# Group-norm statistics from transposed blocks, joined by averaging matrices, and the first relative-position products placed between the keys

## The chip, the cores and the metric

The kernel runs on one core of one Trainium2 chip. A core has five engines that run their own instruction streams: TensorE (matrix products, PE in the profile), VectorE (DVE), ScalarE (ACT), GpSimd (POOL) and SyncE (SP), which here issues all the DMA transfers. Working memory (SBUF) has 128 partitions; matrix products land in eight accumulation banks (PSUM). The metric is the device time of one execution in microseconds (us); lower is better. All data are 32-bit floats.

## The reference, cut to what matters

Two images of 48x48 tokens and 768 channels go through an attention layer and then a spectral layer, each behind a group norm of 32 groups of 24 channels:

```python
def _gn(v, G=32, eps=1e-5):
    B_, H_, W_, C_ = v.shape
    g = v.reshape(B_, H_, W_, G, C_ // G)
    m = jnp.mean(g, axis=(1, 2, 4), keepdims=True)
    s = jnp.var(g, axis=(1, 2, 4), keepdims=True)
    return ((g - m) / jnp.sqrt(s + eps)).reshape(v.shape)

# attention, inside
attn = jnp.einsum('bqc,bkc->bqk', q * scale, k)
rel_h = jnp.einsum('bhwc,hkc->bhwk', r_q, Rh)
rel_w = jnp.einsum('bhwc,wkc->bhwk', r_q, Rw)
attn = attn + rel_h[..., None] + rel_w[..., None, :]     # shapes shortened
attn = jax.nn.softmax(attn, axis=-1)
...
x = x + _L0_conv_ref(_gn(x), ...)    # attention
x = x + _L1_conv_ref(_gn(x), ...)    # spectral layer
```

The change concerns the first `_gn`, the one ahead of the attention, and the order of the work that follows it.

## The kernel before, in words

`block_kernel` handles the two images one after the other: `attention`, then `project_out` (which also computes the second group norm's statistics), then `Spectral(...).run`. A tile framework orders the instructions, so the start of image 1's `attention` may interleave with the end of image 0's spectral stage (`ps_u`, `ps_x`, the adds `x<-ps_x` at L968, the stores `out<-x` at L971, the round trip `u_d` and `u` through device memory at L940 and L950). Inside `attention`, from L195 on, the engines are wrapped in `InOrder`: what is issued through `pe`, `dve`, `act` and `sync` keeps its program order, and its line in the profile is L66 (the wrapper's), so these rows are told apart by tile names.

`norm_transpose` (L82 to L135) does the first group norm. Six loads bring `x` as six tiles of 128 partitions x 3 token tiles x 768 channels (`xt`, L103). For each of them and each of six channel blocks (`NCC` = 6) TensorE transposes three 128x128 pieces into one bank `gn_tp` (L109), and ScalarE copies the bank into `xnT` (L113), where channels lie on partitions and the 2304 tokens along the row, in an order by quarters (`stretches`). Some banks take two copies of 192 columns in place of one of 384. Beside this, `tile_stats` (L700) computes, for each of the 18 token tiles, the mean of each group of 24 channels (VectorE, L703 and L704), the centred values (GpSimd, L706), their squares (ScalarE, L709) and the sums of squares (VectorE, L710). `join_stats` (L713) joins tokens and tiles: two products with a matrix of ones (`js_tot`, L720 and L733), some VectorE work on 18x32 columns (`js_off`), square root and reciprocal. `cmask` and `pick` (L119, L123) spread the 32 group values to the 128x6 channel layout, and 18 instructions of 768 columns (L128) normalise `xnT` in place.

After that, `attention` loads the first weights (`load_w`; the third shares its buffer with the second), and computes for head pair 0 the queries of token group 0 (`queries`), six parts of the keys (`keys`), the relative products of group 0 (`relative`: `ps_r`, copied to `rel`), writes them skewed to device memory and reads them back (`write`, `read`: tiles `t` and `rhw`), the queries of group 1, and then the first unit (`new_unit`: GpSimd spreads the two relative terms over the 2304 keys in a tile `s`, one instruction for each of the two heads, L320). The main loop runs over units (head pair, group, third): `scores` (products `ps_s`, added into `s` by VectorE with a running maximum), `numerators` (ScalarE's exponential), transposes and DMA exchanges to `pT`, `weigh` (`ps_o`), with keys and values of the next head pair in between. `evict` writes out what waits on ScalarE.

The few lines that carry the first order of work after the norm:

```python
qT = queries(0, 0)
evict(by_act)
for i in range(6):
    keys(0, i)
    evict(by_act)
rhw, write, read = relative(0, qT)
...
ahead = new_unit(*order[0])
```

A query group needs columns 0 to 1535 of `xnT` for its rows (twelve runs of 32 in the first quarter); a part of the keys needs 384 columns next to each other.

Of the kernel before, what the change touches and what calls it, by code (L numbers as in the profile page):

```python
# [9 lines left out]
F32 = mybir.dt.float32  # L10
AF = mybir.ActivationFunctionType
ALU = mybir.AluOpType
AX = mybir.AxisListType
# [3 lines left out]
P = 128  # L17
HW = 48
S = HW * HW
C = 768  # L20
# [3 lines left out]
NCC = C // P  # L24
NT = S // P
NG = 32
GC = C // NG
# [5 lines left out]
UQ = 384  # L33
# [8 lines left out]
YP = 112  # L42
XP = 4
WP = 5
LAM = 0.01
GN_EPS = 1e-5
LOWEST = -3.0e38
# [21 lines left out]
def stretches(cols, g):  # L69


    by_quarter = cols.rearrange("p (t c j) -> p t c j", c=4, j=32)
    e = 0
    while e < UQ:
        c, t = divmod((g * UQ + e) // 32, NKC)
        n = min(NKC - t, (UQ - e) // 32)
        yield e, e + 32 * n, by_quarter[:, t : t + n, c, :]
        e += 32 * n
# [3 lines left out]
def norm_transpose(nc, k, pools, bank, x_b, xnT):  # L82

    tiles, small, work, a = pools
    k.load(nc, a, small, {"cmask": [P, NCC, NG]})
    local = small.tile([P, NT, NG], F32, tag="local", name="local")  # L90
    dev = small.tile([P, NT, NG], F32, tag="dev", name="dev")
    src = x_b.rearrange("(t p) c -> p t c", p=P)
    loaded = []
    for i in range(NT // 3):
        if i < 2:
            xt = tiles[0].tile([P, S], F32, tag="x", name="xt")
        elif i % 2 == 0:
            both = tiles[1].tile([P, 2, S], F32, tag="s", name="xt")
            xt = both[:, 0, :]
        else:  # L100
            xt = both[:, 1, :]
        xt = xt.rearrange("p (t c) -> p t c", c=C)
        nc.sync.dma_start(out=xt, in_=src[:, 3 * i : 3 * i + 3, :])  # L103
        loaded.append(xt)
    for t0, xt in zip(range(0, NT, 3), loaded):
        for cc in range(NCC):
            tp = bank("gn_tp")
            for i in range(3):
                nc.tensor.transpose(  # L109
                    tp[:, i * P : (i + 1) * P], xt[:, i, cc * P : (cc + 1) * P], k.ident  # L110
                )
            for e0, e1, dst in stretches(xnT[:, cc, :], t0 // 3):
                nc.scalar.copy(dst, tp[:, e0:e1].rearrange("p (t j) -> p t j", j=32))  # L113
        for i in range(3):
            tile_stats(nc, work, xt[:, i, :], local[:, t0 + i, :], dev[:, t0 + i, :])
    cols = []
    for i, stat in enumerate(join_stats(nc, k, small, bank, local, dev)):
        m = small.tile([P, NCC, NG], F32, tag="pick", name="pick")
        nc.vector.tensor_tensor(  # L119
            m, k.cmask, stat[:, None, :].to_broadcast([P, NCC, NG]), ALU.mult  # L120
        )
        c = small.tile([P, NCC], F32, tag=f"gcol{i}", name=f"gcol{i}")
        nc.vector.tensor_reduce(c, m, AX.X, ALU.add)  # L123
        cols.append(c)
    for c0 in range(0, S, 2 * UQ):
        for cc in range(NCC):
            xs = xnT[:, cc, c0 : c0 + 2 * UQ]
            nc.vector.tensor_scalar(  # L128
                xs,
                xs,  # L130
                cols[0][:, cc : cc + 1],
                cols[1][:, cc : cc + 1],
                ALU.subtract,
                ALU.mult,
            )  # L135


# [1 line left out]
def attention(tc, k, x_b, a, oT, inv_d, late, span, ps_b, ps_o):  # L139
# [10 lines left out]
    nc = tc.nc  # L150
    with ExitStack() as ctx:
# [11 lines left out]
        sp = pool("at_s", 3)  # L163
# [19 lines left out]
        rel = relp.tile([P, 2, 3, 2, RW], F32, tag="rel", name="rel")  # L183
        with ExitStack() as ctx2:
            small = ctx2.enter_context(tc.tile_pool(name="gn_s", bufs=1))
            work = lambda name: small.tile([P, C], F32, tag="st", name=name, bufs=2)
            more = ctx2.enter_context(tc.tile_pool(name="gn_x", bufs=2))
            norm_transpose(nc, k, ((more, sp), small, work, a), bank, x_b, xnT)
        ptp = pool("at_pt", 2)
        b_cols = a["qkv_b"].rearrange("(j p) -> p j", p=P)  # L190
        with nc.allow_non_contiguous_dma(reason="biases onto partitions"):
# [21 lines left out]
        by_act, by_dve = [], []  # L213

        def evict(waiting):
            while waiting:
                waiting.pop(0)()
# [234 lines left out]
        groups, weights, kTs, vs = {}, {}, {}, {}  # L452
        for which in (0, 1):
            weights[which] = load_w(which, 0)
        qT = queries(0, 0)
        evict(by_act)
        for i in range(6):
            keys(0, i)
            evict(by_act)
        rhw, write, read = relative(0, qT)  # L460
        evict(by_act)
        write()
        read()
        groups[0, 0] = (qT, rhw)
        weights[2] = load_w(2, 0)
        staged = ((0, 1), queries(0, 1))
        evict(by_act)
        ahead = new_unit(*order[0])
        recent = []
        last = turn = send = None  # L470
        for n in range(len(order) + 3):
# [228 lines left out]
def tile_stats(nc, work, xt, local, dev):  # L700

    x3 = xt.rearrange("p (g d) -> p g d", d=GC)
    nc.vector.tensor_reduce(local, x3, AX.X, ALU.add)  # L703
    nc.vector.tensor_scalar(local, local, 1.0 / GC, None, ALU.mult)  # L704
    xc = work("st_xc").rearrange("p (g d) -> p g d", d=GC)
    nc.gpsimd.tensor_tensor(  # L706
        xc, x3, local[:, :, None].to_broadcast([xt.shape[0], NG, GC]), ALU.subtract
    )
    nc.scalar.activation(xc, xc, AF.Square)  # L709
    nc.vector.tensor_reduce(dev, xc, AX.X, ALU.add)  # L710


def join_stats(nc, k, small, bank, local, dev):  # L713

    ntok = float(S)
    rows, tiles = local.shape[:2]
    part = small.tile([rows, NG], F32, tag="js_part", name="js_part")
    nc.vector.tensor_reduce(part, local.rearrange("p t g -> p g t"), AX.X, ALU.add)
    tot = bank("js_tot")
    nc.tensor.matmul(tot[:, :NG], lhsT=k.ones[:rows, :], rhs=part, start=True, stop=True)  # L720
    mean = small.tile([P, NG], F32, tag="js_mean", name="js_mean")
    nc.vector.tensor_scalar(mean, tot[:, :NG], 1.0 / ntok, None, ALU.mult)
    off = small.tile([rows, tiles, NG], F32, tag="js_off", name="js_off")
    nc.vector.tensor_tensor(
        off, local, mean[:rows, None, :].to_broadcast([rows, tiles, NG]), ALU.subtract
    )
    nc.vector.tensor_tensor(off, off, off, ALU.mult)
    nc.vector.tensor_scalar(off, off, float(GC), None, ALU.mult)
    nc.vector.tensor_tensor(off, off, dev, ALU.add)
    part2 = small.tile([rows, NG], F32, tag="js_part", name="js_part2")  # L730
    nc.vector.tensor_reduce(part2, off.rearrange("p t g -> p g t"), AX.X, ALU.add)
    tot2 = bank("js_tot2")
    nc.tensor.matmul(tot2[:, :NG], lhsT=k.ones[:rows, :], rhs=part2, start=True, stop=True)  # L733
    std = small.tile([P, NG], F32, tag="js_std", name="js_std")
    nc.scalar.activation(std, tot2[:, :NG], AF.Sqrt, bias=k.eps, scale=1.0 / (ntok * GC))
    rstd = small.tile([P, NG], F32, tag="js_rstd", name="js_rstd")
    nc.vector.reciprocal(rstd, std)
    return mean, rstd
# [3 lines left out]
class Spectral:  # L742
# [50 lines left out]
    def bank(self, name):  # L793
        return self.ps_b.tile([P, 512], F32, tag="b", name=name)
# [278 lines left out]
def shape_constants():  # L1073

    h = np.arange(HW)
    full = 2 * np.pi * ((h[:, None] * h[None, :]) % HW) / HW
    half = full[:, :KW]
    s = 1.0 / np.sqrt(HW)

    order = np.concatenate([h[0::2], h[1::2]])  # L1080

    fw = np.zeros((2, HW, KW, 2, 2))
    for i in range(2):
        fw[i, :, :, 0, i], fw[i, :, :, 1, i] = np.cos(half) * s, -np.sin(half) * s
    fw = np.concatenate([fw.reshape(2 * HW, 4 * KW), np.zeros((2 * HW, YP - 4 * KW))], 1)

    co, si = np.cos(full), np.sin(full)
    fh = np.block([[co[order], -si[order]], [si[order], co[order]]]) * s

    ih = np.zeros((2, HW, 2, 2, HW // 2))  # L1090
    for i in range(2):
        c2, s2 = co[:, i::2] * s, si[:, i::2] * s
        ih[0, :, i, 0], ih[1, :, i, 0] = c2, -s2
        ih[0, :, i, 1], ih[1, :, i, 1] = s2, c2
    ih = np.pad(ih.reshape(2, HW, 2 * HW), ((0, 0), (0, 64 - HW), (0, 0))).reshape(P, 2 * HW)

    m = np.full((KW, 1), 2.0)
    m[0] = m[-1] = 1.0
    sin = np.sin(half).T.copy()
    sin[0] = sin[-1] = 0.0  # L1100
    iw = np.zeros((KW, 2, 2, 2, HW))
    for i in range(2):
        iw[:, i, 0, i], iw[:, i, 1, i] = m * np.cos(half).T * s, -m * sin * s
    iw = iw.reshape(4 * KW, 2 * HW)
    gmask = np.arange(BS)[:, None] // GC == np.arange(4)[None, :]
    cmask = (np.arange(C).reshape(NCC, P).T // GC)[:, :, None] == np.arange(NG)
    named = {"cmask": cmask, "fh": fh, "fw": fw, "ih": ih, "iw": iw, "gmask": gmask}
    return {n: np.ascontiguousarray(v, dtype=np.float32) for n, v in named.items()}


# [47 lines left out]
```

## Time and profile before

| what | time in us |
|---|---|
| median of three runs | 3907.91 (3903.24 to 3908.79) |
| profiled execution, its own time | 3910.83 |
| its span in the profile | 3908.9 |
| image 0: first x tile used, last statistics joined, first projection, second score add | 8.0, 54.0, 59.84, 107.23 |
| image 1: first x load issued, first projection, second score add | 1923.25, 2010.48, 2057.03 |
| VectorE busy in 8 to 20 us | 12.00 of 12.00 |
| TensorE busy in 45 to 60 us | 1.38 of 15.00 |

The page of the profile gives the busy time of each engine, the span in 40 slices (a digit is the busy share in tenths), the chain of work that ended last, and the costliest groups of instructions. An "idle before" in a row is what the engine waited for. The chain of waits lists, in order of time, which engine or transfer held up the end at each point. A matrix product of 32-bit floats shows as two records.

### The profile page before, as it was taken

To read this page: it belongs to the slowest core of one execution; us is meant where nothing else is said; L and a number is where in the kernel's file an instruction comes from. 1 tells how busy PE (TensorE), PEld (TensorE's weight loads), DVE (VectorE), ACT (ScalarE), POOL (GpSimd) and SP (SyncE) were. 2 spreads that over 40 slices of the span, in tenths; PEclk is the share of its full clock that TensorE was granted. 3 is DMA by queue.
4 is the path that set the end of the run, shared out by engine and by line. 5 is a ranking of instruction groups with operands and counts; after the bars stand their busy time and mean duration, and the time that the engine had idled before them with its cause. 6 is when DMAs were issued, how large, how long until landed. Compare 5 with 4: busy or idle time off the path is not lost.

```text
span 3908.9 us, 83210 instructions
## 1 busy us (share of the span) xinstructions
PE 3660.4 (94%) x31416; PEld 2591.6 (66%) x31416; DVE 2987.5 (76%) x6642; ACT 2528.1 (65%) x3585; POOL 2117.0 (54%) x682
## 2 busy tenths in 40 slices
PE   6999999999999888989959999999999999779898
PEld 4677776767777655566536777767677776545665
DVE  5688888888889885654546888888888888856544
ACT  3588888888888882222135888888888888722221
POOL 2566666666666666422225666666666666664221
PEclk7999999999999998999989999999999999989999
DMA  2477777777777888534424777777777778884344
GB/s 93 100 169 172 171 175 165 170 172 174 173 167 166 175 197 197 130 84 122 139 85 104 176 171 170 168 174 168 172 172 167 176 164 177 189 197 127 85 121 131
DMA packets 496094, 606.22 MB, mean 155 GB/s; under 512 B 180109, under 2 KB 311053, under 8 KB 495694
## 3 DMA queue, kind: packets, MB, share of 16 engines
q1 hardware_dynamic: 495694, 600.89, 66.1%
q8 instruction: 250, 4.10, 0.5%
q14 instruction: 150, 1.23, 0.1%
HBM read 130.81 MB, written 87.67 MB: 56 GB/s over the span
## 4 chain that ended last, share of the span: by engine, by line
PE 80%; DVE 6%; DMA 6%; POOL 4%; SPq 3%; issue 1%; ACT 1%; POOLq 0%; DVEq 0%; ACTq 0%
PE ps_o L66 20%; PE ps_s L66 19%; PE ps_proj L66 14%; PE ps_v L66 8%; PE acc L670 5%; DVE s L66 4%; PE ps L905 4%; POOL s L320 2%; SPq L66 2%; DMA pT<-s 2%; PE ps_z L853 2%; PE ps L878 2%; PE ps L882 2%; PE ps_u L936 2%; PE ps_r L66 1%
## 5 line engine op out<-in xcount | busy, mean ns | idle before, releaser
L320 POOL TENSOR_TENSOR s<-rhw 128x2304 f32<-128x2304 f32 x432 | 1744.8, 4060 | 1096.4 <-DMA pT<-s 575.9
L66 DVE CUSTOM_DVE_ANT_0 s<-ps_s,s 128x512 f32<-128x512 f32 (+1 forms) x2160 | 1223.3, 633 | 401.0 <-issue 225.6
L66 ACT ACTIVATE s<-s,nm 128x1152 f32<-128x1152 f32 x864 | 1074.7, 1245 | 445.9 <-DVE nm L66 415.1
L66 DVE STREAM_TRANSPOSE s<-s 128x1152 f32<-128x1152 f32 x864 | 1111.8, 1344 | 5.5 <-ACT s L66 5.5
L66 ACT COPY pT<-s 32x1152 f32<-32x1152 f32 x864 | 993.2, 1149 | 28.8 <-PE ps_o L66 13.3
L66 PE MATMUL ps_o<-pT,v 128*64 128x128 f32 x15552 | 924.5, 279 | 77.7 <-DMA pT<-s 41.7
L66 PEld LDWEIGHTS ps_o<-pT,v 128*64 128x64 f32 x15552 | 872.7, 140 | 140.6 <-issue 79.0
L66 PE MATMUL ps_s<-kT,qT 64*128 64x512 f32 (+1 forms) x4320 | 922.4, 559 | 23.2 <-DVE mx L66 19.3
L66 PEld LDWEIGHTS ps_s<-kT,qT 64*128 64x128 f32 x4320 | 432.5, 187 | 462.6 <-issue 335.6
L66 PE MATMUL ps_proj<-xnT,w 128*128 128x384 f32 (+1 forms) x2016 | 597.4, 450 | 11.8 <-issue 11.8
L66 PEld LDWEIGHTS ps_proj<-xnT,w 128*128 128x128 f32 x2016 | 360.5, 191 | 219.2 <-DVE mx L66 41.1
L670 PE MATMUL acc<-proj 128*128 128x384 f32 x864 | 291.6, 497 | 24.5 <-POOL proj L616 12.4
L66 PEld LDWEIGHTS ps_v<-w,xnT 128*128 128x128 f32 x2592 | 297.6, 194 | 21.8 <-DVE mx L66 21.8
L66 PE MATMUL ps_v<-w,xnT 128*128 128x128 f32 x2592 | 309.8, 279 | 0.0
L922 POOL TENSOR_TENSOR spectrum<-spectrum 128x480 f32<-128x480 f32 x80 | 96.2, 1203 | 326.7 <-DVE spectrum L921 323.9
L670 PEld LDWEIGHTS acc<-proj 128*128 128x128 f32 x864 | 168.0, 195 | 144.6 <-issue 21.3
L709 ACT ACTIVATE st_xc<-st_xc 96x768 f32<-96x768 f32 (+1 forms) x84 | 71.1, 847 | 266.7 <-POOL st_xc L706 266.7
L679 DVE TENSOR_TENSOR x<-acc,x 32x384 f32<-32x384 f32 (+2 forms) x216 | 119.5, 553 | 80.2 <-PE acc L670 76.3
L66 DVE DVE_READ_ACCUMULATOR2_ANT mx<- 128x1 f32 x2160 | 180.1, 83 | 0.0
L66 ACT ACTIVATION_READ_ACCUMULATOR s<-s,nm 128x1 f32 x864 | 161.2, 187 | 0.0
L710 DVE TENSOR_REDUCE dev<-st_xc 96x32 f32<-96x768 f32 (+1 forms) x84 | 78.9, 948 | 96.4 <-ACT st_xc L709 96.4
L706 POOL TENSOR_TENSOR st_xc<-x,local 96x768 f32<-96x768 f32 x48 | 70.9, 1481 | 148.2 <-DVE local L704 128.8
(87 smaller groups left out, 2275.1 us busy)
## 6 DMA issues: line engine op xcount, KB each, us to landing
pT<-s SPq DMA_DIRECT2D x2592, 144.0 KB
t<-rel SPq DMA_DIRECT2D x144, 189.0 KB
rhw<-t SPq DMA_DIRECT2D x144, 144.0 KB
y_d<-y SPq DMA_DIRECT2D x24, 672.0 KB
y<-y_d SPq DMA_DIRECT2D x40, 360.0 KB
u_d<-spectrum SPq DMA_DIRECT2D x40, 360.0 KB
u<-u_d SPq DMA_DIRECT2D x48, 300.0 KB
xt<-in_x SPq DMA_DIRECT2D x12, 1152.0 KB
```

The source lines that it names most:

```text
L66: return lambda *args, **kw: self.tc.keep_in_program_order(op(*args, **kw))
L320: nc.gpsimd.tensor_tensor(s[:, h, :].rearrange("p (y x) -> p y x", x=HW), rhw[:, x, h, :HW][:, :, None].to_broadcast([P, HW, HW]), rhw[:, ...
L670: nc.tensor.matmul(acc[:, :UQ], lhsT=o_sb[:, cc, (t % 3) * P : (t % 3 + 1) * P], rhs=pr.w[:, cc, cols], start=(cc == 0), stop=(cc == NCC - 1),
L679: nc.vector.tensor_tensor(dst, acc[p : p + n, :UQ], dst, ALU.add)
L709: nc.scalar.activation(xc, xc, AF.Square)
L710: nc.vector.tensor_reduce(dev, xc, AX.X, ALU.add)
L853: nc.tensor.matmul(ps[:BS, w * 96 : (w + 1) * 96], lhsT=self.y2[s, j][:, w, i * BS : (i + 1) * BS], rhs=k.fh, start=True, stop=True,)
L878: nc.tensor.matmul(ps[:BS, :400], lhsT=w1[:, wa, i, :], rhs=zf[:, 0, fs], start=True, stop=False,)
L882: nc.tensor.matmul(ps[:BS, :400], lhsT=w1[:, wb, i, :], rhs=zf[:, 1, fs], start=False, stop=True,)
L905: nc.tensor.matmul(ps[64 * r : 64 * r + 64, w * BS : (w + 1) * BS], lhsT=self.o1[:, ri, f0 : f0 + 64], rhs=w2[:, (0, 2, 1, 0)[2 * r + ri], ...
L922: nc.gpsimd.tensor_tensor(val, val, clip, ALU.subtract)
L936: nc.tensor.matmul(ps[: 2 * HW, :480], lhsT=k.ih, rhs=d2[:, c0 : c0 + 480], start=True, stop=True)
```

## The change

The group norm's statistics are no longer taken from the token-major tiles. For each `gn_tp` bank (128 channels x 384 tokens), VectorE takes one batch-statistics instruction (`bn_stats`), which leaves six numbers for each channel; after six groups, `bn_aggr` joins the six pieces of each channel block to a mean and a variance. `by_group` joins channels to groups: a constant `same` holds seven 128x128 matrices with 1/24 where two channels are of one group; seven products of two columns average the channels' means, and again their variances plus squared offsets. Square root and reciprocal follow, on 128x6 values that already lie by channel, so `cmask` and `pick` go. The normalising instructions take 384 columns each (36 of them), all channel blocks of one stretch before the next. `same` is loaded behind the x tiles where `cmask` was loaded ahead of them.

In `attention`, the keys start first; the queries of group 0, their relative products, the trip through device memory and the first unit come after the fourth part of the keys, ahead of the fifth and sixth.

```diff
+SAME = ((0, 0), (1, 0), (0, 1), (1, 1), (2, 1), (1, 2), (2, 2))
@@ norm_transpose
-    tiles, small, work, a = pools
-    k.load(nc, a, small, {"cmask": [P, NCC, NG]})
-    local = small.tile([P, NT, NG], F32, tag="local", name="local")
-    dev = small.tile([P, NT, NG], F32, tag="dev", name="dev")
+    tiles, small, a = pools
...
-    for t0, xt in zip(range(0, NT, 3), loaded):
+    k.load(nc, a, small, {"same": [P, 7, P]})
+    pieces = small.tile([P, NCC, NT // 3, 6], F32, tag="pieces", name="pieces")
+    for g, xt in enumerate(loaded):
         for cc in range(NCC):
             tp = bank("gn_tp")
...
-            for e0, e1, dst in stretches(xnT[:, cc, :], t0 // 3):
+            nc.vector.bn_stats(pieces[:, cc, g, :], tp[:, :UQ])
+            for e0, e1, dst in stretches(xnT[:, cc, :], g):
                 nc.scalar.copy(dst, tp[:, e0:e1].rearrange("p (t j) -> p t j", j=32))
-        for i in range(3):
-            tile_stats(nc, work, xt[:, i, :], local[:, t0 + i, :], dev[:, t0 + i, :])
-    cols = []
-    for i, stat in enumerate(join_stats(nc, k, small, bank, local, dev)):
-        m = small.tile([P, NCC, NG], F32, tag="pick", name="pick")
-        nc.vector.tensor_tensor(
-            m, k.cmask, stat[:, None, :].to_broadcast([P, NCC, NG]), ALU.mult
-        )
-        c = small.tile([P, NCC], F32, tag=f"gcol{i}", name=f"gcol{i}")
-        nc.vector.tensor_reduce(c, m, AX.X, ALU.add)
-        cols.append(c)
-    for c0 in range(0, S, 2 * UQ):
+    stat = small.tile([P, NCC, 2], F32, tag="stat", name="stat")
+    for cc in range(NCC):
+        nc.vector.bn_aggr(stat[:, cc, :], pieces[:, cc].rearrange("p g e -> p (g e)"))
+
+    def by_group(cols, name):
+        ps = bank(name)
+        halves = cols.rearrange("p (i m) -> p m i", m=3)
+        for m in range(3):
+            near = [j for j in (m - 1, m, m + 1) if 0 <= j < 3]
+            for j in near:
+                nc.tensor.matmul(
+                    ps[:, 2 * m : 2 * m + 2],
+                    lhsT=k.same[:, SAME.index((j, m)), :],
+                    rhs=halves[:, j, :],
+                    start=(j == near[0]),
+                    stop=(j == near[-1]),
+                )
+        return ps[:, :NCC].rearrange("p (m i) -> p i m", m=3)
...
+    nc.vector.tensor_copy(of_channel, stat[:, :, 0])
+    nc.vector.tensor_copy(as_halves(mean), by_group(of_channel, "gn_mean"))
+    nc.vector.tensor_tensor(off, of_channel, mean, ALU.subtract)
+    nc.vector.tensor_tensor(off, off, off, ALU.mult)
+    nc.vector.tensor_tensor(off, off, stat[:, :, 1], ALU.add)
+    nc.scalar.activation(as_halves(rstd), by_group(off, "gn_var"), AF.Sqrt, bias=k.eps)
+    nc.vector.reciprocal(rstd, rstd)
+
+    for i in range(S // UQ):
         for cc in range(NCC):
-            xs = xnT[:, cc, c0 : c0 + 2 * UQ]
+            xs = xnT[:, cc, i * UQ : (i + 1) * UQ]
             nc.vector.tensor_scalar(
...
@@ attention
-        qT = queries(0, 0)
-        evict(by_act)
         for i in range(6):
             keys(0, i)
             evict(by_act)
-        rhw, write, read = relative(0, qT)
-        evict(by_act)
-        write()
-        read()
-        groups[0, 0] = (qT, rhw)
+            if i == 3:
+                qT = queries(0, 0)
+                evict(by_act)
+                rhw, write, read = relative(0, qT)
+                evict(by_act)
+                write()
+                read()
+                groups[0, 0] = (qT, rhw)
+                ahead = new_unit(*order[0])
         weights[2] = load_w(2, 0)
         staged = ((0, 1), queries(0, 1))
         evict(by_act)
-        ahead = new_unit(*order[0])
@@ shape_constants
-    cmask = (np.arange(C).reshape(NCC, P).T // GC)[:, :, None] == np.arange(NG)
+    group = np.arange(C // 2).reshape(3, P) // GC
+    same = np.stack([group[j][:, None] == group[m][None, :] for j, m in SAME], 1) / GC
```

More of the change, by code (lines that the diff above doesn't have):

```diff
@@ new lines, in column @@
+    def column(name):
+        return small.tile([P, NCC], F32, tag=name, name=name)
+    of_channel, mean, off, rstd = (column(f"gn_{n}") for n in ("ch", "mean", "off", "rstd"))
+    as_halves = lambda t: t.rearrange("p (i m) -> p i m", m=3)
+    nc.vector.tensor_copy(of_channel, stat[:, :, 0])
[3 more added lines that the diff above has]
+    nc.vector.tensor_tensor(off, off, stat[:, :, 1], ALU.add)
@@ L126, in norm_transpose @@
+    nc.scalar.activation(as_halves(rstd), by_group(off, "gn_var"), AF.Sqrt, bias=k.eps)
+    nc.vector.reciprocal(rstd, rstd)
+    for i in range(S // UQ):
         for cc in range(NCC):
-            xs = xnT[:, cc, c0 : c0 + 2 * UQ]
+            xs = xnT[:, cc, i * UQ : (i + 1) * UQ]
             nc.vector.tensor_scalar(
[L129 to L134, printed above, removed]
+                xs, xs, mean[:, cc : cc + 1], rstd[:, cc : cc + 1], ALU.subtract, ALU.mult
@@ L185, in attention @@
             small = ctx2.enter_context(tc.tile_pool(name="gn_s", bufs=1))
-            work = lambda name: small.tile([P, C], F32, tag="st", name=name, bufs=2)
             more = ctx2.enter_context(tc.tile_pool(name="gn_x", bufs=2))
-            norm_transpose(nc, k, ((more, sp), small, work, a), bank, x_b, xnT)
+            norm_transpose(nc, k, ((more, sp), small, a), bank, x_b, xnT)
         ptp = pool("at_pt", 2)
@@ L1105, in shape_constants @@
     gmask = np.arange(BS)[:, None] // GC == np.arange(4)[None, :]
-    cmask = (np.arange(C).reshape(NCC, P).T // GC)[:, :, None] == np.arange(NG)
-    named = {"cmask": cmask, "fh": fh, "fw": fw, "ih": ih, "iw": iw, "gmask": gmask}
+    group = np.arange(C // 2).reshape(3, P) // GC
+    same = np.stack([group[j][:, None] == group[m][None, :] for j, m in SAME], 1) / GC
+    named = {"same": same, "fh": fh, "fw": fw, "ih": ih, "iw": iw, "gmask": gmask}
     return {n: np.ascontiguousarray(v, dtype=np.float32) for n, v in named.items()}
```

## The prediction

> **What bounds the kernel now.** I read the page's parts 1, 2 and 4 first, then the chain of waits over the start of each image (0 to 420 us and 1880 to 2120 us), then the timeline and the stretches of the same places.
>
> ```profile
> PE 3660.4 (94%) x31416; PEld 2591.6 (66%) x31416; DVE 2987.5 (76%) x6642; ACT 2528.1 (65%) x3585; POOL 2117.0 (54%) x682
> PE   6999999999999888989959999999999999779898
> PE 80%; DVE 6%; DMA 6%; POOL 4%; SPq 3%; issue 1%; ACT 1%; POOLq 0%; DVEq 0%; ACTq 0%
> ```
>
> TensorE is busy almost everywhere except slice 1 (image 0 begins) and slice 20 (image 1 begins). The change edits just these two places. From the chain of waits (start, us, what):
>
> ```profile
> 44.61 1.10 DVE js_part L718
> ...
> 59.84 30.36 PE ps_proj L66 x84
> 90.19 0.92 PE ps_r L66 x12
> 91.11 0.84 ACT rel L66 x2
> 91.97 0.75 SPq L66
> 92.78 3.73 DMA t<-rel
> 96.57 2.44 DMA rhw<-t
> ...
> 103.15 4.06 POOL s L320
> 107.23 0.69 DVE s L66
> ...
> 1963.57 7.57 DMA xt<-in_x
> ...
> 1996.66 1.14 DVE js_part L718
> ...
> 2010.48 29.55 PE ps_proj L66 x84
> ```
>
> The reader is to see three stages in each image, and in image 1 that stage A ends 33 us after the last x loads are issued. A: from the first x tile to js_part, a VectorE-GpSimd-ScalarE relay, 8.0 to 44.6 us. B: joining and normalising, 44.6 to 59.84, with TensorE idle. C: 30 us of projections, then a serial tail, relative products, copy, two DMA hops, GpSimd's sums, before VectorE may add the second score piece at 107.23 (2057.03 in image 1). After that TensorE works through values and scores without regard to what came before.
>
> The timeline prices the parts:
>
> ```profile
> 11.51 1.80 DVE L703 TENSOR_REDUCE local<-xt 128x32 f32<-128x768 f32 x2
> 20.89 2.37 ACT L113 COPY xnT<-gn_tp 128x384 f32<-128x384 f32 x6
> 45.84 0.61 PE L720 MATMUL js_tot<-js_part,ones 128*128 128x32 f32 x2 [11.49 <-DVE js_part L718]
> 55.52 10.70 DVE L128 TENSOR_SCALAR xnT<-xnT,gcol,gcol 128x768 f32<-128x768 f32 x18
> ```
>
> [...] In the changed program each ScalarE copy of a gn_tp bank indeed waits for VectorE's statistic of that bank[...]. [...] the trace has 0.52 to 0.56 for the v copy 128x384. [...] granted 0.50 in 45 to 60 us.
>
> **Stage A.** Removed: per token tile two VectorE reductions (0.86 us apart each) and a scaling, GpSimd's 1.49, ScalarE's 0.85, a relay that takes 36.6 us for 18 tiles. Added: 36 statistics of 128x384 from PSUM. The nearest rows are the adds x<-ps_x, 11 of 96x384 in 5.18 us, 0.47 each[...]. Floor 0.47[...]. I take 0.47.
>
> Image 0: x moves at about 405 GB/s (stretches 8 to 20), so 7.08 MB end at about 21.4 us, one tile of three per 2.9 us; six statistics take 2.8, six ScalarE copies 2.4 to 2.8, so all three keep step. Transposes take 0.21 each at first, three to a bank, 0.64 a bank: the first six banks end at 11.6, the other 30 at 0.48 bring 26.3. The new constant `same` (448 KB, 1.1 us of transfer) is queued behind x and is there by then; the weights behind it move by that 1.1 us, from about 25 to 26, and are needed after 35. Free.
>
> Image 1: in before, the first x load waits for the last second-layer product (L905) and is issued at 1923.25, beside the stores of u; VectorE then stands 3.79 us on it with the last adds of image 0 behind it, and the norm's reductions interleave with those adds. In the changed program both first loads and `same` wait for the last ps_z product, the point where cmask was issued, 1894.31, and DMA is idle from 1900 to 1915; all statistics stand behind the 24 adds. So: last u copies at 1929 instead of 1932, 12 adds to 1935 (1937.4), u loads issued at 1935.6 (1939.47), landed at 1940.2 (1945.17), 24 ps_x of 10.3 us and the last add at 1951 (1956.96), output stored and the last four x loads issued at 1957 (1962.96). 5.9 us earlier; bounds 0 to 6. The first 12 statistics fill that wait. The four loads take 11.5 us after a latency of 2.3: last at 1970.8, then six banks and the backlog, 1975.5. In before the same point, js_part, is 1996.66.
>
> **Stage B**, new, from the last statistic: six aggregations of 36 numbers (nearest: gcol's reduction, 0.26 apart; I take 0.3, bounds 0.1 to 0.6) 1.8; copy and the bias scaling 0.3; hop 0.1; seven matmuls of two columns, 14 passes: js_tot gives 0.2 between its two passes cold, a warm pass about 0.1, so 1.3 to 3.2, taken 2.2; copy and three tiny VectorE operations 0.7; the second seven 2.2; square root 0.35, reciprocal 0.3; first normalising step 0.45 with its hop 0.1. Sum 8.5. In image 0 the program puts the wait for the matmuls ahead of the table load, which in before stood under the reductions (48.41), so 1.28 comes onto the path: 9.8. In image 1 the load has no wait in front and stays covered.
>
> The normalising steps become 36 of 384 columns. 18 took 0.595 each; half of the moving part and the same fixed part give about 0.39, 14.2 us in all against 10.7. Hidden: the first keys need six steps (2.4 us) for 3.87 us of products, and now begin after the first step, where queries waited for the seventh (4.3 us after the start).
>
> ps_proj then begins at 26.3 + 9.8 = 36.1 (59.84): 23.7 us. Image 1: 1975.5 + 8.5 = 1984.0 (2010.48): 26.5 us.
>
> **Stage C.** Before, ps_r stands 30.3 us after the start of ps_proj (seven groups). Now two keys, 2 x 3.87, come later; but ps_r follows directly on its queries and TensorE waits for ScalarE's qT, 0.58 and hops: 0.75. So ps_r comes at 30.3 - 7.74 + 0.75, 7.0 us earlier. Everything from ps_r to the second add keeps its 17.1 us: two copies, t issued (two DMAs), rhw (two DMAs), GpSimd twice 4.06. Beneath it TensorE now has two keys 7.7, queries 4.2 and 3.7 of scores, where it had the last two only and stood idle for most of 98.8 to 107.98. On SP, t and rhw now go ahead of the third weight load, which waits for the last key; it lands at about 35 us into the stage, and values begin at 43. GpSimd and the other units follow as before. Gain 7.0 an image; bounds 0 and 7.7.
>
> **Sum.** 23.7 + 26.5 + 7.0 + 7.0 = 64.2 us. The profiled execution took 3910.83 us (span 3908.9 and 1.93 around it): 3846.6. It lies 2.9 above the median of the runs, 3907.91; on that footing 3843.7, so **3844**.
>
> **Rivals.**
> - [...] 36 more exposed in image 0 and 24 in image 1, 60 x 0.4 = 24 us, 3868. For: the statistics gather mean and squares in one pass and no row shows them. [...]
> - Stage C hidden: the transfer or GpSimd is late anyway, or the stall on qT and the queues eat the 7 us. 14 us less, 3858. Against: the chain of waits passes through each of these with nothing beside it.
> - Better: the transposes now run without pauses and leave TensorE at full clock for the small matmuls (four times 1.1) and the first projection, whose half clock costs 3.2 us (first group 7.1, the others 3.87): 4.4 + 6.4 = 10.8, 3833. Against: stage B still leaves TensorE idle for over 3 us in all.
> - The other side: the statistics as several passes. The gain is gone from 1.45 us each: 36 x 0.98 in image 0, 24 x 0.98 in image 1, and there the first 12 outgrow their 12.4 us wait by 5. [...]
>
> **How the numbers follow.** Forecast 0.65, half rate 0.12, C hidden 0.10, better 0.08, slower 0.05. The range is 3833 to 3868: from the better case to half-rate statistics; it also holds the small terms' bounds (aggregations -2.4 to +3.6 and matmuls -3.6 to +4 over both images). 0.2%, 8 us, is what a measurement tells apart here: faster 0.94, same 0.01, slower 0.05.
>
> **What would show it.** Statistics of about 0.47 to 0.53 us back to back, the last near 26 us; ps_proj at about 36 and 1984; an ACT table load just ahead of the square root in image 0; x loads at 1894 in image 1 with no VectorE wait at 1926 to 1930; the second score add 40 us after ps_proj's start, with less than 3 us of idle TensorE before it. A statistic above 0.8, small matmuls above 0.3 a pass, or a TensorE idle stretch of over 6 us in stage C would make it wrong.

## The result, and the profile after

| | before | after |
|---|---|---|
| median of five runs, us | 3907.91 (3903.24 to 3908.79) | 3845.90 (3839.75 to 3850.62) |
| ratio, with its 95% interval | | 0.9846 (0.9833 to 0.9860) |
| profiled execution / its span, us | 3910.83 / 3908.9 | 3845.32 / 3843.2 |
| granted TensorE clock in it | 0.967 | 0.974 |

The changed kernel is faster by about 62 us by the medians (the ratio gives 60, with 55 to 65 as its interval). From the page of the changed kernel, parts 1, 2 and 4:

```profile
PE 3661.7 (95%) x31464; PEld 2599.0 (68%) x31464; DVE 2950.0 (77%) x6642; ACT 2502.4 (65%) x3549; POOL 2063.9 (54%) x646
...
PE   8999999999999988989989999999999999779898
...
PE 81%; DMA 6%; DVE 5%; POOL 4%; SPq 2%; issue 1%; ACT 1%; POOLq 0%; DVEq 0%; ACTq 0%
```

TensorE does as much as before (3661.7 against 3660.4 us busy) in a shorter span. Two slices have changed by more than a tenth: the first went from 6 tenths to 8, and the one in which image 1 begins, the 21st (the prediction calls it slice 20), from 5 to 8; the 14th went from 8 to 9. The chain of waits over the start of image 0 (start, length in us, what; three dots stand for rows left out; rows of 0.1 us and less are left out without a mark):

```profile
7.63 5.37 PE gn_tp L111 x24
13.02 13.59 DVE pieces L114 x29
26.61 1.10 DVE stat L119 x6
...
28.16 3.13 PE gn_mean L129 x14
...
32.23 3.13 PE gn_var L129 x14
...
35.44 1.28 ACT L148
36.73 0.28 ACT gn_rstd L148
...
37.84 22.60 PE ps_proj L67 x60
60.46 0.59 ACT qT L67
61.09 0.99 PE ps_r L67 x12
...
73.99 4.07 POOL s L340
78.08 0.69 DVE s L67
```

The relay of three engines is gone: one row of statistics (`pieces`) leads straight to the aggregation at 26.61, two sets of seven small products (14 records each, a product being two records) follow with TensorE otherwise idle, and the projections start at 37.84, where they started at 59.84. Four keys and the queries then go ahead of the relative products (60 records in place of 84), and the second score add comes at 78.08, 40.24 us into the projections (47.39 before). This last length, from the start of the projections to the second score add, is stage C. The same view where image 1 begins:

```profile
1919.88 3.79 DMA out<-x
1923.72 5.70 DMA xt<-in_x
...
1934.94 8.00 DVE pieces L114 x17
1942.94 1.11 DVE stat L119 x6
...
1944.39 2.48 PE gn_mean L129 x14
...
1947.81 3.13 PE gn_var L129 x14
...
1950.97 0.28 ACT gn_rstd L148
...
1952.13 21.20 PE ps_proj L67 x60
...
1991.31 0.69 DVE s L67
```

The last x loads wait for the output of image 0, as before, but the last statistic now ends 19.2 us after they begin (1923.72 to 1942.94). In the kernel before, `js_part` stood 33 us behind them.

Lengths taken within one trace add up to the measured gain. In image 0 the projections start 22.0 us earlier and stage C is 7.2 shorter. For image 1, take a fixed point in the second layer of image 0, the first of its last 48 `ps_x` records (1928.01 before, 1895.10 after). From there to the projections the way falls from 82.47 to 57.03, 25.4 us, and stage C from 46.55 to 39.18, 7.4. The sum is 62.0. That the medians differ by exactly this is chance, since the interval of the ratio spans 10 us. The spans of the two profiled executions differ by 65.7; the other 3.8 us arise between the second score add of image 0 and the fixed point, where no edit lies. That stretch lasts 1820.8 us before and 1817.0 after, and between 1817.0 and 1827.0 in the ten traces of this document, so its length varies by more than this from one execution to the next.

### The profile page after: what moved, and what is told of

Read it like the earlier page. It is cut to its first block, busy times and chain, and to the rows that moved or that the text cites. A ratio compares the mean times of both kernels' runs of the same rounds, so it can differ in the third digit from the quotient of the medians.

```text
span 3843.2 us, 83225 instructions
## 1 busy us (share of the span) xinstructions
PE 3661.7 (95%) x31464; PEld 2599.0 (68%) x31464; DVE 2950.0 (77%) x6642; ACT 2502.4 (65%) x3549; POOL 2063.9 (54%) x646
## 4 chain that ended last, share of the span: by engine, by line
PE 81%; DMA 6%; DVE 5%; POOL 4%; SPq 2%; issue 1%; ACT 1%; POOLq 0%; DVEq 0%; ACTq 0%
PE ps_o L67 20%; PE ps_s L67 19%; PE ps_proj L67 14%; PE ps_v L67 8%; PE acc L691 5%; DVE s L67 4%; PE ps L926 4%; POOL s L340 3%; DMA pT<-s 2%; SPq L67 2%; PE ps_z L874 2%; PE ps_u L957 2%; PE ps_x L981 2%; PE ps L899 2%; PE ps L903 2%; PE ps_r L67 1%
## 5 line engine op out<-in xcount | busy, mean ns | idle before, releaser
L730 ACT ACTIVATE st_xc<-st_xc 96x768 f32<-96x768 f32 x48 | 40.5, 843 | 234.6 <-POOL st_xc L727 234.6
L907 ACT ACTIVATE spectrum<-ps,b 96x400 f32<-96x400 f32 x96 | 56.5, 589 | 140.1 <-PE ps L903 140.1
```

## Experiments

Each kernel is the changed one with the edit named, but for the third, which is the kernel before with one edit. Ratios are to the kernel before, run on the same chip (median 3912.8 us beside the first four, 3913.31 beside the others). Microseconds of a ratio are (1 - ratio) times the median of before; those of the changed kernel itself are 60.2. Stage lengths are from each kernel's own trace.

**1. The new statistics with the old order of work.** Queries first, relative products behind all six keys, the first unit behind the second queries:

```
+        qT = queries(0, 0)
+        evict(by_act)
         for i in range(6):
             keys(0, i)
             evict(by_act)
-            if i == 3:
...
+        rhw, write, read = relative(0, qT)
...
```

> The new statistics with the old order of queries, keys and relative products. My theory: the order is worth about 14 us an image, in two halves. The queries need 19 of the 36 normalising steps at 0.39 us where the keys need one, so ps_proj starts 6.9 us later; and ps_r stands 30.3 us behind that start in place of 23.3, so the second score add comes another 7.1 us later. Together 28 us, 3874. Rival 1, only the relative chain counts and the start is hidden: 14 us, 3860. Rival 2, the statistics carry the whole gain and the order is free: 3846.

Measured 3880.24 us, ratio 0.9918 (0.9905 to 0.9932): 32.1 us faster than before, so 28.1 us short of the change. Its chain of waits in image 0:

```profile
26.46 1.10 DVE stat L119 x6
...
35.47 0.27 ACT gn_rstd L148
...
43.59 30.37 PE ps_proj L67 x84
73.96 0.92 PE ps_r L67 x12
...
91.16 0.69 DVE s L67
```

There are two losses in it. Stage C is back at 47.57 us (40.24). And 8.1 us pass between the start of the square root and the first projection, where the changed kernel has 1.1: the first product of the queries reads columns of four parts, and since the statistics part of the change has cut normalising into 36 steps of 0.39 us, it waits for the 19th of them (7.4 us). In image 1 the same gap is 8.2 us against 1.2. Over both images, counted as above, the way to the second add is 28.6 us longer, which agrees with the 28.1. So together with the new statistics the move is worth about 28 us, half of it through the shorter wait for the normalised columns.

**2. Relative products behind the last key, queries after the sixth.** `if i == 3:` becomes `if i == 5:`.

> Keys still first, but queries, relative products and first unit after the sixth part of the keys. My theory: ps_proj starts as in the changed kernel (37.8 in image 0), ps_r comes two keys, 7.74 us, later, and the second score add moves from 40.2 to 48 us behind that start: 15.5 us over both images, 3861. Rival, the chain is hidden behind TensorE's own work: 3846, the second add stays at about 40.

Measured 3867.71 us, ratio 0.9885 (0.9871 to 0.9898): 15.2 us slower than the change. Its chain in image 0:

```profile
28.26 1.71 PE gn_mean L129 x14
...
36.51 29.16 PE ps_proj L67 x84
...
83.45 0.69 DVE s L67
```

The second add comes 46.94 us after the start of the projections in image 0 and 46.90 in image 1 (40.24 and 39.18): 14.4 us in all. Two keys behind the relative products in place of ahead of them are worth 7.2 us per image on average, and nothing else takes their place.

**3. The move alone**, on the norm of before (the new order of experiment 1's diff, in the other direction).

> The norm of the kernel before with the changed order of keys and relative products. My theory: the first keys wait for one normalising step of 768 columns in place of the seventh (3.7 us) and the relative chain gains 7.1, so 10.8 us an image, 3886. Rival 1, only the chain: 7 us an image, 3894. Rival 2, the move helps only together with the new statistics: 3908.

Measured 3888.26 us, ratio 0.9942 (0.9929 to 0.9954): 22.7 us faster. Its chain in image 0:

```profile
45.10 1.10 DVE js_part L719
...
54.51 0.29 ACT js_std L736
...
56.78 20.98 PE ps_proj L66 x60
...
95.54 0.69 DVE s L66
```

The old statistics still end at 45, but the projections start 3.1 us earlier than before (56.78 against 59.84), since a key waits for fewer normalised columns than the queries. The second add is 8.6 us closer to them (38.76). With image 1 (4.2 and 7.4) that makes 23.3 us. Rival 1, which gives the move the serial tail alone, 14 us, is too small: the interval is 18 to 28 us.

**4. The x loads of image 1 put back to their late time.** A large tile nobody reads, in the pool of the small tiles, keeps the first loads behind the last of image 0's spectral work:

```
+    pad = small.tile([P, 2600], F32, tag="pad", name="pad")
+    nc.gpsimd.memset(pad[:, 0:1], 0.0)
     k.load(nc, a, small, {"same": [P, 7, P]})
```

> The changed kernel with an unused tile of 10.4 KB a partition, which moves the first two x tiles of image 1 to memory that comes free later, so that their loads again wait for the second layer's products and are issued some 30 us later, beside the stores of u. Theory 1, the early loads give the 5.9 us that I counted for the end of image 0: the last four x loads come 5.9 us later, 3852. Theory 2, VectorE's order (statistics behind the last adds) gives it: under 1 us, 3846. From the stores of u that the x transfers held up I expect about 3 us, 3849; image 0 unchanged.

The rows of SP's queue in its timeline show that the edit does this:

```profile
1898.31 0.80 SPq L103 DMA_DIRECT2D xt<-in_x  x1
...
1902.64 1.29 SPq L103 DMA_DIRECT2D xt<-in_x  x1
...
1934.78 2.48 SPq L103 DMA_DIRECT2D xt<-in_x  x4
```

The first load is issued 4.8 us before the fixed point (1903.07 in this trace), as in the kernel before (35.0 before it in the changed one). The last four loads come 31.7 us after that point: 28.6 in the changed kernel, 34.9 before. So of the 6.3 us by which the change brings them forward, 3.1 come from the earlier first loads, and 3.2 remain without them. That remainder is what the other half of the prediction's reason would leave: the statistics stand behind the last adds of image 0 and no longer among them; this was not tried by itself. The projections of image 1 start 3.3 us later than in the changed kernel. The time, 3850.35 us, ratio 0.9838 (0.9824 to 0.9851), doesn't differ from the change's; 3 us are too few for it to tell, so the gain is seen in a single pair of traces alone.

**5. Each statistic taken twice**, the first copy into a tile that isn't used:

```
+    spare = small.tile([P, 6], F32, tag="spare", name="spare")
...
+            nc.vector.bn_stats(spare, tp[:, :UQ])
             nc.vector.bn_stats(pieces[:, cc, g, :], tp[:, :UQ])
```

> Each batch statistic is taken twice, the first into a spare tile. My theory: VectorE's 36 statistics at 0.50 us set the end of stage A in image 0, 36 x 0.5 = 18 us more; in image 1 the last 24 are exposed, 12 us, and the first 12 fit the wait for the last x loads (12.4 us): 30 us, 3876. Rival, the transfers of x or TensorE's transposes set the pace and half of the statistics' time is cover: 15 us or less, 3861.

Measured 3877.88 us, ratio 0.9907 (0.9894 to 0.9921): 23.8 us slower than the change. The last of VectorE's statistics in image 0, from its timeline:

```profile
41.21 0.55 DVE L115 BATCH_NORM_STATS2 spare<-gn_tp 128x6 f32<-128x384 f32 x1
41.67 0.55 DVE L116 BATCH_NORM_STATS2 pieces<-gn_tp 128x6 f32<-128x384 f32 x1
42.14 1.18 DVE L121 BATCH_NORM_AGGREGATE stat<-pieces 128x2 f32<-128x36 f32 x6
```

Each record lasts 0.55 us, but one starts 0.46 to 0.47 us after another: the spacing, 0.465 on average over the rows ahead, is the price. The projections start 15.6 us later in image 0, where 36 x 0.465 = 16.7 were added, and 10.4 later in image 1, where 24 fall behind the last adds (11.2). Nearly all of the added time is exposed, so VectorE sets stage A. The 1.1 us missing in image 0 were covered by the slower transposes of the first banks: in the changed kernel the 36 statistics take 18.1 us (8.54 to 26.61), 1.3 more than 36 x 0.465, with `gn_tp` on the chain up to 13.0, while the 72 here follow one another without a gap.

**6. Queries and relative products after the second key**, `if i == 1:`.

> Queries, relative products and first unit after the second part of the keys in place of the fourth. My theory: ps_r comes 7.74 us earlier, but then TensorE's own work sets the first scores: seven groups 30.3, the wait for qT 0.7, ps_r 0.9, the second queries 4.2, so the second add comes at about 36.9 us behind ps_proj's start in place of 40.2: 3.3 us an image, 3839. Rival 1, the chain still sets it: 7.7 us an image, 3830. Rival 2, the four keys were already cover enough: 3846.

Measured 3839.83 us, ratio 0.9811 (0.9798 to 0.9825): 13.8 us below the change by the ratios, give or take about 7. From the projections up to 108 us the chain of waits of image 0 now runs through TensorE, apart from the copy of `qT` (0.59):

```profile
37.90 14.71 PE ps_proj L67 x36
...
53.26 0.94 PE ps_r L67 x12
54.20 19.58 PE ps_proj L67 x72
73.78 4.07 PE ps_s L67 x20
```

The relative products come 15.36 us after the projections start (23.25), 7.9 earlier, but the second add only 2.5 and 2.7 us: the add is no longer late because of the tail, it waits for TensorE's own work. With the tail hidden under 19.6 us of projections, the chain leaves nothing to gain from moving the products further forward; that was not tried. The ratio shows more than these 5.2 us, which lie just outside its interval. The traces don't show where the rest would come from, and it stays open.

**7. One join in place of two.** The aggregated variance plus the squared mean is the mean square; mean and mean square are joined in one set of seven products of four columns. A square root at the very start brings the activation table in:

```
+        nc.scalar.activation(k.warm, k.eps, AF.Sqrt)
...
-    nc.vector.tensor_copy(as_halves(mean), by_group(of_channel, "gn_mean"))
...
+                ps[:, 4 * m : 4 * m + 4],
+                lhsT=k.same[:, SAME.index((j, m)), :],
+                rhs=halves[:, j],
```

> Channel mean and mean square (variance plus squared mean) are averaged over the group in one set of seven products of four columns in place of two sets of two, and a square root of one element at the very start loads ScalarE's table in image 0. My theory: one set of 3.1 us and its hops go, 3.3 us an image, and the table load's 1.28 us in image 0: 7.9 us, 3838; ps_proj at about 33.2 in image 0. Rival, a pass of four columns costs twice one of two, or the clock sinks: 3845.

ScalarE's only table load ahead of the scores of image 0, from its timeline, and the chain of waits there:

```profile
0.74 1.28 ACT L108 ACT_TABLE_LOAD   x1 [0.74 <-PEq L1166]
...
26.59 1.10 DVE stat L122 x6
...
28.34 3.04 PE gn_join L132 x14
...
32.02 0.31 ACT gn_rstd L144
...
33.16 22.34 PE ps_proj L67 x60
```

Measured 3843.59 us, ratio 0.982 (0.9807 to 0.9833): 10 us below the change, give or take about 7. The traces have the projections 4.7 us earlier in image 0 and 3.1 in image 1, of which 4.7 and 2.6 lie behind the last statistic. The second set of products and its VectorE steps lay wholly on the path. Behind the last statistic image 0 gains 2.1 us more than image 1. The table load (1.28), which only image 0 had on its path, is the larger part of it; most of the rest is the first set, which took longer in image 0 of the changed kernel (3.13 against 2.48). Join and table load were not tried apart. Fourteen passes (records) of four columns take 3.04 us, as fourteen of two do (3.13): in these two traces the price is by the pass.

**8. Experiment 7 with queries after the second key and relative products after the third.**

```
-            if i == 3:
+            if i == 1:
                 qT = queries(0, 0)
                 evict(by_act)
+            if i == 2:
                 rhw, write, read = relative(0, qT)
```

> The one join and the early table load, with queries after the second part of the keys and the relative products after the third, so that TensorE does not wait for qT. If the parts add: 7.9 us, 3.3 us an image, and the 0.67 us wait for qT an image: 15.8 us, 3830. If the earlier chain brings nothing, 3837.

```profile
31.56 0.31 ACT gn_rstd L144
...
32.70 17.29 PE ps_proj L67 x48
49.98 0.87 PE ps_r L67 x12
50.85 15.71 PE ps_proj L67 x60
```

In this chain no engine but TensorE stands from 32.70 to 101 us, and with a key between the queries and their use the wait for `qT` is gone. Measured 3833.86 us (3830.48 to 3839.85), ratio 0.9797 (0.9784 to 0.9811), which lies below the change's interval: the fastest of the ten kernels here. By the traces, counted as above, the way to the second add is 13.2 us shorter than the change's over both images; the ratios say 19, give or take about 7.

## Why the prediction was right

3844 was forecast and 3845.9 measured, and each of the four terms of the sum (23.7, 26.5, 7.0, 7.0) agrees with the traces within two microseconds. So the mechanism was right. That the total came so close is in part luck: the runs of the changed kernel alone spread over 11 us, and errors of either sign cancelled in part in stage B.

- **Stage A.** The statistics were taken at 0.47 us each; experiment 5 shows 0.465. The last ends at 26.61 in image 0 (26.3). That they are the bound of this stage, experiment 5 shows. In image 1 the first loads stand 35.0 us ahead of the fixed point, where the forecast 1894.31 would be 33.7, and the last loads came 6.3 us earlier (5.9). Half of that is the place of the first loads, by experiment 4; that the other half comes from the order of VectorE's work is argued.
- **Stage B.** This held the mis-sized terms. The seven products were taken at 2.2 us a set. The second set takes 3.13 in both images, 0.22 for each of its 14 passes, at a granted clock of 0.50 (32.20 to 35.40 and 1947.81 to 1950.94). The first takes 3.13 in image 0 (granted 0.50 from 28.10 to 31.30) and 2.48 in image 1 (0.64 from 1944.39 to 1946.87). The aggregations were taken at 0.3 each and follow one another at 0.18, 1.1 in place of 1.8. The rest, table load (1.28) included, came out within 0.3 us. Stage B is 11.2 us in image 0 (9.8 forecast) and 9.2 in image 1 (8.5), so the projections start at 37.84, not 36.1. A gain of 23.7 was forecast there and 22.0 came; in image 1 it was 26.5 and 25.4.
- **Stage C.** 7.0 was forecast per image, 7.2 and 7.4 came. Experiments 1 and 2 take this gain away again. In image 0 TensorE idles 0.67 us for `qT` (0.75 forecast) and 1.33 ahead of the score products that wait for the second add, together below the 3 us set as the mark.

```profile
61.09 0.94 PE L67 MATMUL ps_r<-rel,qT 64*128 64x126 f32 x12 [0.67 <-ACT qT L67]
...
78.83 1.31 PE L67 MATMUL ps_s<-kT,qT 64*128 64x256 f32 x4 [1.33 <-DVE mx L67]
```

These are TensorE's rows in the timeline of the changed kernel; the bracket has the idle time before the row and who ended it.

The rivals: half-rate statistics and several passes fall with the 0.465 us. The 0.4 us more for each of 60 statistics was the author's estimate; the trace of before gives about the same, since its score adds of 512 elements follow one another at 0.61 us and its adds of 384 (`x<-ps_x`) at 0.47, which makes an estimated 0.42 for 384 elements more. The hidden stage C falls with experiment 2, which puts the 15 us back by moving two keys alone. The better case, full clock for the small products and the first projection, falls with the stretches of the changed kernel (stretch, its length, then busy time of PE, PEld, DVE, ACT, POOL with instruction counts, the granted clock, DMA share, GB/s):

```profile
26.60:37.80 11.20, 6.24 (x28) 6.12 (x28) 2.70 (x16) 2.07 (x4) 0.00 (x0) 0.51 0.01 2
37.80:61.00 23.20, 22.58 (x60) 12.81 (x60) 13.57 (x35) 2.86 (x5) 0.00 (x0) 0.87 0.00 0
```

The granted clock is 0.51 over the stretch of the small products. It was 1.00 from 8.00 to 26.60, then 0.57 from 26.60 to 28.10, the end of the 3.63 us for which TensorE stood idle ahead of the first set, and 0.50 while either set ran. The projections start cold, that is at half clock: 0.50 from 37.80 to 41.00, 0.64 from 41.00 to 45.00, and 1.00 from 45.00 to 61.00. In image 1, where the idle time ahead of the first set was 2.88 us, the clock was 1.00 from 1941.50 to 1944.39 and fell in the first set (0.64). What sets the moment of the fall was not shown. A small part of the better case does occur: in experiment 2 the first set of image 0 took 1.71 us, 0.12 a pass. Experiment 7 shows how to gain there in another way, by having one set in place of two.

## What to carry to other kernels

Where an idle stretch is bounded by a relay between engines, look for a tile that the stage makes anyway and from which one engine can take the whole statistic, and price it by the spacing of the nearest row with the same source and width (here adds at 0.47 us, and the statistics came at 0.465). Small products with few columns cost by the pass here (0.22 us with two columns at a granted clock of 0.50, and 0.22 with four in experiment 7); halve their number by joining several quantities in one product. When finer steps replace coarse ones, put the consumer that needs few of them first: starting with the keys brings image 0's projections forward by 7.0 us with 36 fine steps (experiment 1) and by 3.1 with 18 coarse ones (experiment 3). For the rest the two parts of the change nearly add: the move alone gave 22.7 us, the new statistics alone 32.1, both together 60.

## What the hardware showed that was not expected

- Batch statistics of 128x384 from PSUM follow one another at 0.465 us with records of 0.55. The records of the v copies of 128x384, 0.52 to 0.56 in the trace of before, lie near the record; the spacing, which counts in a row, is shorter than the record by 0.09.
- An aggregation of 36 numbers per partition starts 0.18 us after the one before it, with a record of 0.26, where the record of a copy of six numbers is 0.17.
- The same 60 records at the start of the projections took 22.60 us here, 22.34 in experiment 7 and 21.02 in experiment 5, where 60 at 0.323 (3.87 for twelve) are 19.4. So the time lost at this point varies by about 1.6 us among executions with the same products. In the changed kernel the granted clock was 0.87 over the stretch above; that the clock makes the difference in the other two was not shown. The first set of small products varies likewise: 1.71 and 2.02 us in image 0 of experiments 2 and 1, 3.13 here and in experiment 6. A stage measured from a cold start carries this scatter.
